# The end of a two-layer transformer kernel: last chunk's stages ahead of the batches, result places computed in the last score steps, dense units turned a step later

## The chip, the cores and the metric

The kernel runs on one core of one Trainium2 chip. The metric is device time in microseconds (us) of one execution. The engines are named as in the profile: PE (TensorE matmul), PEld (its weight loads), DVE (VectorE), ACT (ScalarE), POOL (GpSimd) and SP (SyncE, which here issues most DMAs). Each engine works through its own instructions in the order in which the program lists them, and waits at an instruction until its inputs and its buffer are there.

## The reference

The input x has 32 sequences of 256 tokens with 128 features. Two layers follow. Each has a self-attention with 16 heads of 8, and then a mixture of 16 experts of which every token takes the best two; layer norms are modulated per sequence, and each half is gated per sequence and added to x. Cut to the second layer's expert part, which the change concerns:

```python
h = layernorm(x) * (1 + cb) + sb
probs = softmax(h @ router_w.T)                 # 16 experts
top_w, top_i = top_k(probs, 2); top_w /= sum(top_w)
for e in range(16):                             # 64 wide
    out += dense_w[:, e] * ((silu(h @ Wg[e]) * (h @ Wu[e])) @ Wd[e])
out += sigmoid(h @ shared_gate_w) * ((silu(h @ Sg) * (h @ Su)) @ Sd)   # 256 wide
x = x + gb * out
```

Everything is computed in float32.

## The kernel before

The 32 sequences are cut into 16 chunks of two sequences (512 tokens). Two layers make 32 chunks of work, C = 0 to 31; C from 16 on is layer 1. The program is one long loop over steps `t`, written out by hand. A chunk takes 16 steps, in which its attention scores are formed twice (for the maxima, and 12 steps later for the exponentials) and multiplied by the values. The scores end at step `NU` = 512; the loop runs on to `END`, which is about 70 steps later.

Within each step the program emits instructions in a fixed order: score and value matmuls; early planned work (`early`); the stages of the chunk that fall on this place in its 16 steps, for the engines other than PE (`on_others`, then `on_others_late`); planned work that comes behind (`behind_`); the chunk's stage on PE (`on_pe`); and late planned work (`late`), which is mostly PE's. `plan(at, where, f, ...)` puts a call into one of the three planned lists. So the position of a call within a step is its position in each engine's queue.

The stages of a chunk after its scores are, on the non-PE side: copy of the values' product (`copy_pv`, ACT), division by the softmax sums (`divide`, DVE: rec L981 and cx L983), `keep_ctx` (ACT L998), `add_o` (DVE L1013), statistics and norm (`stats`, `norm`, ACT L551), the modulation (`h_rows`, POOL L614 and L616), `keep_h` (ACT L637), and the routing. On PE they alternate with `turn_ctx` (cT, L989), `proj_o` (y, L1003), `turn_b` (xnT_b, L563) and `logits` (lp, L643).

The experts' work is sparse for most chunks. Tokens are scattered by expert into an array `hs` in HBM, by groups of chunks (8, 8, 8 and 6 chunks; the last group is chunks 24 to 29). Each group is then worked off in batches of four tiles of 128 rows: load the rows (`load`, SP L1315), turn them (t, L1358), multiply by the up weights (gu, L1371), activation (`act_1`, ACT L1394, DVE L1395 and L1396), turn again (aT, L1414), copy (`keep_act`, ACT L1418), multiply by the down weights (y, L1425), weigh (yw, DVE L1436) and store to `ys` (SP L1443). The last group has 16 batches, one in each step from about 511, in the order turn, up, down, turn_act on PE. When all of a group is stored, POOL gathers each token's two rows back with indirect DMAs (L855, eight for a chunk), from places that `find_slots` computes on DVE: L817 twice, L823, L830 and L832, which writes the tile gslot. The sums are gated and added to x (`y_summed` L870, `y_gated` L874, `y_added` L878) and stored (L1642). The gate is loaded by SP into a single buffer (yg, L800).

The two last chunks, 30 (`DENSE`) and 31 (`LAST`), go another way: all experts are computed for all their tokens, as 40 units (2 chunks, 4 token tiles, 5 parts: four of four experts each, and the shared expert). The units begin two steps before the last batch is done. A unit has a product on PE (`dense_up`, du, L1471 or L1474) into one of four banks, a tanh (ACT L1489), three DVE operations (L1490, L1492, L1493, or L1490 and L1495 for the shared part), a turn on PE (`dense_turn`, L1499) back into its bank, a copy (`dense_keep`, ACT L1505) and the down product (`dense_down`, L1514). `dense_add` (L1525, L1526) adds a finished token tile to x and SP stores it (L1528).

Of the kernel before, what the change touches and what calls it, by code (L numbers as in the profile page):

```python
# [9 lines left out]
F32 = mybir.dt.float32  # L10
U32 = mybir.dt.uint32
# [6 lines left out]
B, S, D = 32, 256, 128  # L18
H, HD = 16, 8
E, FI, FS = 16, 64, 256  # L20
EPS = 1e-5
P = 128
# [3 lines left out]
NT = CT // P  # L26
# [4 lines left out]
G, J, R = 2, 8, 16  # L31
# [50 lines left out]
def two_layers(  # L82
# [37 lines left out]
    work = ctx.enter_context(tc.tile_pool(name="work", bufs=2))  # L120
    once = ctx.enter_context(tc.tile_pool(name="once", bufs=1))
    small = ctx.enter_context(tc.tile_pool(name="small", bufs=2))
# [11 lines left out]
    groups = [Group(k) for k in range(len(GROUPS))]  # L134
# [10 lines left out]
    early, behind_, late = {}, {}, {}  # L145

    def plan(at, where_, f, *args):
        where_.setdefault(at, []).append((f, args))
# [238 lines left out]
    def where(C):  # L387

        return divmod(C, NCHUNK)

    def group_of(C):
        return next((g for g in groups if g.first <= C < g.end), None)
# [12 lines left out]
    NU = CHUNKS * CB * G * 4  # L405
# [399 lines left out]
    shifts, gslots = {}, {}  # L805
# [6 lines left out]
    def find_slots(C):  # L812

        l, c = where(C)
        oh = small.tile([P, 2, NT, E], F32, tag="oh2", bufs=1, name=f"oh2_{C}")
        for n in range(2):
            nc.vector.tensor_tensor(  # L817
                oh[:, n],
                iota_e,
                chosen[:, c, :, n : n + 1].to_broadcast([P, NT, E]),  # L820
                ALU.is_equal,
            )
        nc.vector.tensor_tensor(  # L823
            oh,
            oh,
            shifts[group_of(C).k].unsqueeze(1).unsqueeze(1).to_broadcast([P, 2, NT, E]),
            ALU.mult,
        )
        sh = small.tile([P, 2, NT], F32, tag="sh", name=f"sh_{C}")
        nc.vector.tensor_reduce(sh, oh, AX.X, ALU.add)  # L830
        gslots[C] = small.tile([P, 2, NT], U32, tag="gslot", bufs=8, name=f"gslot_{C}")
        nc.vector.tensor_tensor(gslots[C], sh, rowed[:, c], ALU.add)  # L832

    yt2s, gathered_from = {}, {}
# [266 lines left out]
    def do(t, what, dc, *rest):  # L1101
        C = t // 16 + dc
        if 0 <= C < CHUNKS:
            what(C, *rest)
# [346 lines left out]
    UNITS = [(C, t, part) for C in range(DENSE, CHUNKS) for t in range(NT) for part in range(5)]  # L1451
# [24 lines left out]
    def dense_act(n):  # L1476
        C, t, part = UNITS[n]
        p = dn_ps[n]
        s = once.tile([P, G, S], F32, tag="cu", name=f"ds{n}").rearrange("p g s -> p (g s)")[:, :FS]
        a_ = work.tile([P, G, S], F32, tag="q2", name=f"da{n}").rearrange("p g s -> p (g s)")[:, :FS]  # L1480
        dn_as[n] = a_
        if part < 4:
            gu = p.rearrange("p (e n i) -> p e n i", n=2, i=FI)
            gate, upv = gu[:, :, 0, :], gu[:, :, 1, :]
            s, a_ = (v.rearrange("p (e i) -> p e i", i=FI) for v in (s, a_))
            w = everyone[C][:, t, 4 * part : 4 * part + 4].unsqueeze(2).to_broadcast([P, 4, FI])
        else:
            gate, upv = p[:, :FS], p[:, FS:]
        nc.scalar.activation(s, gate, AF.Tanh, scale=0.5)  # L1489
        nc.vector.scalar_tensor_tensor(a_, s, 1.0, gate, ALU.add, ALU.mult)  # L1490
        if part < 4:
            nc.vector.tensor_tensor(a_, upv, a_, ALU.mult)  # L1492
            nc.vector.tensor_tensor(a_, a_, w, ALU.mult)  # L1493
        else:
            nc.vector.scalar_tensor_tensor(a_, a_, zts[C][:, t, :], upv, ALU.mult, ALU.mult)  # L1495
# [153 lines left out]
    END_ROOM = (2, 2, 2, 2, 2, 2, 1, 0, 1, 0, 0, 2, 2, 2, 2, 2)  # L1649
    END = 0  # L1650

    at, left = 16 * (CHUNKS - 3) + 4, 0
    for g in groups:
        if g.l == 0:
            continue
        if at < done[g.k] + 2:
            at, left = done[g.k] + 2, 0
        for C in range(g.first, g.end):
            plan(NU + 2 * (C - g.first) if g is groups[-1] else at, behind_, find_slots, C)
            for n in range(8):  # L1660
                while left == 0:
                    at += 1
                    if at < NU:
                        left = ROOM[at % 16]
                    else:
                        left = END_ROOM[at - NU] if at < NU + len(END_ROOM) else 1 + (at % 5 == 0)
                left -= 1
                if n == 0:
                    gathered_from[C] = at
                plan(at, behind_, gather, C, n)  # L1670
            plan(at, behind_, y_gate, C)
            later = 6 if g is groups[-1] else 3
            plan(at + later - 1, behind_, y_summed, C)
            plan(at + later, behind_, y_gated, C)
            plan(at + later + 1, behind_, y_added, C)
            plan(at + later + 2, early, store, C)
            END = max(END, at + later + 3)

    plan(16 * LAST + 2, early, pairs_weights)
    R0, D0 = 16 * (LAST + 1) + 13, done[groups[-1].k] - 2  # L1680
    plan(16 * (LAST + 1) + 5, behind_, dense_gates, DENSE)
    plan(D0, behind_, dense_gates, LAST)
    for n in range(len(UNITS) + 4):
        for f, where_, after in (
            (dense_turn, late, 2),
            (dense_down, late, 3),
            (dense_up, late, 0),
            (dense_keep, early, 3),
            (dense_act, early, 1),
        ):  # L1690
            if 0 <= n - after < len(UNITS):
                plan(D0 + n, where_, f, n - after)
        if n >= 4 and UNITS[n - 4][2] == 4:
            plan(D0 + n, early, dense_add, *UNITS[n - 4][:2])
    END = max(END, D0 + len(UNITS) + 4)
    for at, where_ in ((0, early), (0, behind_), (1, early), (1, early), (1, behind_), (1, behind_)):
        plan(R0 + at, where_, lambda: next(routes[LAST]))

# [46 lines left out]

    for t in range(-AHEAD, END):
        place = t % 16
        if t == NU:
            scores_pool.__exit__(None, None, None)
            endp.append(ctx.enter_context(end_pool))  # L1750
        m2, after2 = weigh_parts(t) if 0 <= t < NU else ([], None)

        if t < 0:
            if t % 2 == 0:
                (m1, after1), (m2, held_back) = (
                    maxima_parts(
                        t + n + AHEAD, pair(f"s1_{t + n + AHEAD}") if n else None
                    )
                    for n in range(2)
                )  # L1760
            else:
                m1, after1 = [], held_back
        else:
            m1, after1 = maxima_parts(t + AHEAD) if t + AHEAD < NU else ([], None)
        for n in range(NQ):
            for out_, lhs, rhs in m1[2 * n : 2 * n + 2] + m2[2 * n : 2 * n + 2]:
                nc.tensor.matmul(out_, lhs, rhs, start=True, stop=True)  # L1767
        if place in on_pe_mid:
            do(t, *on_pe_mid[place])
        then = [others(p) for others, p in after_job]  # L1770
        after_job.clear()
        for f, args in early.get(t, ()):
            f(*args)
        for stage in on_others.get(place, ()):
            if t < 0 and (stage[0], t // 16 + stage[1]) == (keep_v, 0):
                continue
            do(t, *stage)
        if after1:
            after1()
        if after2:  # L1780
            after2()
        for f in then:
            if f:
                f()
        for stage in on_others_late.get(place, ()):
            if t < 0 and stage[0] in (stats, power, offset) and t // 16 + stage[1] == 1:
                continue
            do(t, *stage)
        for f, args in behind_.get(t, ()):
            f(*args)  # L1790
        if 2 <= t <= NU + 1:
            values(t // 2 * 2 - 1, t % 2)
        if place in on_pe and not (t < 0 and on_pe[place][0] is proj_v):
            do(t, *on_pe[place])
        for g in groups:

            if t == 16 * (g.end + 1) + 1:
                jobs[:0] = table_jobs(g)
        if place == 12 and NCHUNK <= t // 16 - 1 < DENSE:
            jobs.extend(shared_jobs(t // 16 - 1))  # L1800
        for f, args in late.get(t, ()):
            f(*args)
        if t >= NU and jobs or t >= 0 and jobs and t % 3 == 0:
            name, pe, others = jobs.pop(0)
            p = bank("a", name) if t < NU else end_bank(3, name)
            pe(p)
            after_job.append((others, p))
# [102 lines left out]
```

## Time and profile before

| what | time |
|---|---|
| median of 3 runs | 1776.97 us (1776.05 to 1781.66) |
| the profiled execution | 1783.62 us |
| its span, first to last instruction | 1781.9 us |
| mean granted TensorE clock | 0.972 |
| PE busy | 1679.8 us (94%) |
| DVE busy | 1343.5 us (75%) |
| ACT busy | 971.6 us (55%) |
| POOL busy | 717.7 us (40%) |

The rest of the numbers come from one profiled execution, with times counted from its first instruction. A line of the timeline shows the start, the time from the first start to the last end of the merged instructions, the engine, the line of the kernel, the operation, its output and inputs with shapes, and how many were merged. In brackets stands the idle time of the engine just before, and what ended it. A line by stretches shows the stretch, its length, the busy time and the number of instructions of PE, PEld, DVE, ACT and POOL, the granted TensorE clock, the busy share of the DMA engines and what they moved in GB/s. The chain that ended last is followed back from the last instruction, at each step to what released it.

### The profile page before, as it was taken

What the parts mean: (1) busy time and instruction counts of PE and PEld (TensorE: products, weight loads), DVE (VectorE), ACT (ScalarE), POOL (GpSimd) and SP (SyncE); (2) the same over time, 40 slices, a digit from 0 to 9 for tenths busy, and PEclk for the clock granted to TensorE, in tenths of its full rate; (3) what the DMA queues carried; (4) which work ended last, traced back from release to release, by engine and by line L of the source; (5) the groups of instructions that cost most, each with busy time, mean ns of one, the idle gap of its engine ahead of it and who ended that gap; (6) DMA issues with size and microseconds to landing.
All of it is one profiled execution on the core that took longest, in us unless ns stands there. A gap on an engine that the chain in (4) does not pass through costs nothing.

```text
span 1781.9 us, 45990 instructions
## 1 busy us (share of the span) xinstructions
PE 1679.8 (94%) x17025; PEld 1040.6 (58%) x17025; DVE 1343.5 (75%) x3811; ACT 971.6 (55%) x1602; POOL 717.7 (40%) x697
## 2 busy tenths in 40 slices
PE   7999999999999999999999999999999999998897
PEld 3555555555656665555666665555656666546754
DVE  6677777777768877786888887888776767755677
ACT  2566666666546666664546555655665455543333
POOL 2013333332212335664334344555543343553374
PEclk9999999999999999998999999999999999978899
DMA  2132112112445432223444544122332331234532
GB/s 58 41 77 67 47 49 63 49 45 63 105 108 126 106 91 57 56 59 79 111 112 114 95 96 103 45 50 63 99 85 74 81 96 51 69 110 107 139 93 81
DMA packets 211137, 143.38 MB, mean 80 GB/s; under 512 B 33410, under 2 KB 195618, under 8 KB 210914
## 3 DMA queue, kind: packets, MB, share of 16 engines
q1 hardware_dynamic: 187954, 108.65, 24.5%
q0 software_dynamic: 22528, 31.61, 7.1%
q8 instruction: 138, 2.26, 0.5%
q14 instruction: 85, 0.69, 0.1%
q10 hardware_dynamic: 432, 0.16, 0.0%
HBM read 76.91 MB, written 44.62 MB: 68 GB/s over the span
## 4 chain that ended last, share of the span: by engine, by line
PE 42%; DVE 13%; ACT 3%; issue 2%; DMA 2%; POOL 1%; SPq 0%; DVEq 0%; POOLq 0%; ACTq 0%
PE s L1767 14%; PE pv L1186 6%; DVE mpad L1150 3%; PE y L1425 3%; PE gu L1371 3%; PE su L1550 1%; PE aT L1414 1%; PE so L1567 1%; PE t L1358 1%; PE lp L643 1%; PE sg L1539 1%; PE vp L950 1%; PE tp L971 1%; ACT ex L1174 1%; DVE yw L1436 1%
## 5 line engine op out<-in xcount | busy, mean ns | idle before, releaser
L1174 ACT ACTIVATE ex<-s 128x1024 f32<-128x1024 f32 x512 | 523.4, 1022 | 473.9 <-PE s L1767 471.1
L1150 DVE TENSOR_REDUCE mpad<-s 128x2 f32<-128x512 f32 x1018 | 656.9, 688 | 159.1 <-PE s L1767 156.3
L1767 PE MATMUL s<-ka,qa 32*128 32x256 f32 x4096 | 639.4, 414 | 20.5 <-DVE mpad L1150 18.5
L1767 PE MATMUL s<-qa,ka 32*128 32x256 f32 x4096 | 591.2, 406 | 6.6 <-DMA qa<-mc 3.6
L1767 PEld LDWEIGHTS s<-ka,qa 32*128 32x128 f32 x4096 | 376.5, 189 | 198.4 <-DVE mpad L1150 75.1
L1767 PEld LDWEIGHTS s<-qa,ka 32*128 32x128 f32 x4096 | 357.6, 187 | 31.2 <-ACT ex L1174 15.6
L855 POOL DMA_INDIRECT yt<-ys,gslot x220 | 253.5, 1152 | 206.3 <-DVE gslot L832 68.6
L1186 PE MATMUL pv<-ex,vaug 128*32 128x256 f32 x4096 | 332.9, 397 | 3.2 <-ACT cu L964 1.3
L786 POOL DMA_INDIRECT hs<-hrow,slot x240 | 248.0, 1033 | 199.5 <-DVE yt L874 84.1
L1186 PEld LDWEIGHTS pv<-ex,vaug 128*32 128x32 f32 x4096 | 81.2, 109 | 170.1 <-issue 153.4
L769 POOL TENSOR_TENSOR oh<-oh,at 128x128 f32<-128x128 f32 x30 | 14.7, 490 | 257.3 <-DVE at L767 257.3
L534 POOL TENSOR_TENSOR rstd_a<-ve_a,mhalf 128x4 f32<-128x4 f32 x32 | 33.7, 1054 | 174.7 <-DVE ve_a L527 172.1
L1425 PE MATMUL y<-wdd,aT 65*128 (+1 forms) x608 | 89.5, 291 | 0.7 <-ACT aT L1418 0.7
L1425 PEld LDWEIGHTS y<-wdd,aT 65*128 65x128 f32 (+1 forms) x608 | 77.2, 198 | 17.6 <-issue 12.3
L1364 ACT COPY xT<-t 128x512 f32<-128x512 f32 x76 | 44.4, 584 | 78.7 <-PE t L1358 46.4
L1371 PE MATMUL gu<-wgu,xT 128*128 x608 | 86.1, 288 | 0.0
L1371 PEld LDWEIGHTS gu<-wgu,xT 128*128 128x128 f32 x608 | 79.8, 205 | 0.1
L1418 ACT COPY aT<-aT 64x512 f32<-64x512 f32 x76 | 43.9, 577 | 52.2 <-PE aT L1414 51.1
L614 POOL TENSOR_TENSOR xn_b<-xn_b,bc 128x512 f32<-128x512 f32 x32 | 41.0, 1281 | 73.1 <-ACT xn_b L551 73.1
L607 POOL TENSOR_TENSOR wog<-wo,bc 128x256 f32<-128x256 f32 x32 | 31.7, 989 | 82.7 <-DMA bc<-rows 46.2
L551 ACT ACTIVATE xn_a<-x,off_a,rstd_a 128x128 f32<-128x128 f32 x128 | 56.2, 491 | 12.6 <-DVE off_a L540 12.6
L1436 DVE TENSOR_TENSOR yw<-y,hl 128x512 f32<-128x512 f32 x76 | 52.0, 684 | 9.0 <-PE y L1425 8.7
(226 smaller groups left out, 2227.7 us busy)
## 6 DMA issues: line engine op xcount, KB each, us to landing
hl<-hs SPq DMA_DIRECT2D x304, 64.5 KB
ys<-yw SPq DMA_DIRECT2D x76, 256.0 KB
bc<-rows SPq DMA_DIRECT2D x32, 384.0 KB
bg<-bgt SPq DMA_DIRECT2D x160, 64.0 KB
ka<-kc SPq DMA_DIRECT2D x128, 64.0 KB
qa<-qc SPq DMA_DIRECT2D x64, 128.0 KB
hs<-empty SPq DMA_DIRECT2D x68, 64.5 KB
x<-in_x_dram SPq DMA_DIRECT2D x16, 256.0 KB
```

What stands on the lines that cost most here:

```text
L551: nc.scalar.activation(xns[C, ab][:, t, :], xs[c][:, t, :], AF.Identity, bias=off[:, t : t + 1], scale=rstd[:, t : t + 1],)
L786: ins = nc.gpsimd.indirect_dma_start(out=hs[g.k], out_offset=bass.IndirectOffsetOnAxis(ap=slots[C][:, k, t : t + 1], axis=0), in_=hrows[C] ...
L855: ins = nc.gpsimd.indirect_dma_start(out=(yt2s if apart_ else yts)[C][:, t, :], out_offset=None, in_=ys[g.k], in_offset=bass.IndirectOffse ...
L1150: nc.vector.tensor_reduce(to_, sc_, AX.X, ALU.max, negate=True)
L1174: nc.scalar.activation(ex, sc, AF.Exp)
L1186: nc.tensor.matmul(pvs[C, i][j * W : (j + 1) * W, s, :], vaug[C % 2][:, i * NQ + n, s * ST + j, a, :], ex[:, j % 2, n * S : (n + 1) * S], ...
L1364: nc.scalar.copy(xTs[k, b], pst[k, b])
L1371: nc.tensor.matmul(gus[k, b][:, q, :], xTs[k, b][:, q, :], weights[g.l][0][:, bass.ds(es[k, b][q], P)], start=True, stop=True,)
L1418: nc.scalar.copy(aT[:FI], pst["a", g.k, b][:FI])
L1425: nc.tensor.matmul(yps[k, b][:, q, :], aT[:kk, q, :], weights[g.l][1][:kk, bass.ds(es[k, b][q], P)], start=True, stop=True,)
L1436: nc.vector.tensor_tensor(yws[k, b], yps[k, b], hl[k, b][:, :, H_W : H_W + 1].to_broadcast([P, NT, D]), ALU.mult)
L1767: nc.tensor.matmul(out_, lhs, rhs, start=True, stop=True)
```

## The change

Three things change, and two pools.

First, the result places of the last group. `find_slots` for chunks 24 to 29 was planned at steps 512, 514, ... 522. It is now planned at steps 506 to 511, one each. The pool of gslot tiles grows from 8 to 14.

Second, from step 512 on, the early planned work (the batches', the units' and the last routing) is emitted after the stages of `on_others` instead of ahead of them. Before step 512 the order is as it was.

Third, the units. A unit's turn comes three steps after its product instead of two, its copy and down product four instead of three, and `dense_add` five instead of four. The tile da moves to another pool and has three buffers instead of two. The loop's end moves by one step where the units set it.

No instruction is added or taken away.

```diff
@@ find_slots
-        gslots[C] = small.tile([P, 2, NT], U32, tag="gslot", bufs=8, name=f"gslot_{C}")
+        gslots[C] = small.tile([P, 2, NT], U32, tag="gslot", bufs=14, name=f"gslot_{C}")
@@ dense_act
-        a_ = work.tile([P, G, S], F32, tag="q2", name=f"da{n}").rearrange("p g s -> p (g s)")[:, :FS]
+        a_ = once.tile([P, G, S], F32, tag="q2", bufs=3, name=f"da{n}").rearrange("p g s -> p (g s)")[:, :FS]
@@ the plan of the gathers
-            plan(NU + 2 * (C - g.first) if g is groups[-1] else at, behind_, find_slots, C)
+            plan(NU - 6 + C - g.first if g is groups[-1] else at, behind_, find_slots, C)
@@ the plan of the units
-    for n in range(len(UNITS) + 4):
+    for n in range(len(UNITS) + 5):
         for f, where_, after in (
-            (dense_turn, late, 2),
-            (dense_down, late, 3),
+            (dense_turn, late, 3),
+            (dense_down, late, 4),
             (dense_up, late, 0),
-            (dense_keep, early, 3),
+            (dense_keep, early, 4),
             (dense_act, early, 1),
         ):
             if 0 <= n - after < len(UNITS):
                 plan(D0 + n, where_, f, n - after)
-        if n >= 4 and UNITS[n - 4][2] == 4:
-            plan(D0 + n, early, dense_add, *UNITS[n - 4][:2])
-    END = max(END, D0 + len(UNITS) + 4)
+        if n >= 5 and UNITS[n - 5][2] == 4:
+            plan(D0 + n, early, dense_add, *UNITS[n - 5][:2])
+    END = max(END, D0 + len(UNITS) + 5)
@@ the loop over steps
-        for f, args in early.get(t, ()):
-            f(*args)
+
+        planned = early.get(t, ())
+        if t < NU:
+            for f, args in planned:
+                f(*args)
+            planned = ()
         for stage in on_others.get(place, ()):
             if t < 0 and (stage[0], t // 16 + stage[1]) == (keep_v, 0):
                 continue
             do(t, *stage)
+        for f, args in planned:
+            f(*args)
```

## The prediction

> **What bounds the kernel now.** I read the page first (the busy shares, the clock row, the chain that ended last), then busy time by stretch, then TensorE's own timeline of the last 180 us, then the other engines' timelines around each gap in it. The instruction order of the two kernels on every engine is the same up to step 506 (about 1595 us; steps run to 511 with scores). So only the end can move, and I cut it into stretches. The columns are: length; busy PE, PEld, DVE, ACT, POOL; granted clock; DMA share; GB/s.
>
> ```profile
> 1595.00:1613.40 18.40, 17.84 (x116) 8.84 (x112) 5.12 (x21) 8.02 (x13) 10.56 (x11) 0.74 0.60 152
> 1613.40:1692.50 79.10, 67.49 (x441) 59.09 (x438) 50.93 (x166) 26.30 (x57) 30.62 (x32) 0.81 0.44 119
> 1700.00:1772.00 72.00, 64.98 (x329) 39.36 (x328) 57.85 (x138) 27.93 (x77) 47.75 (x48) 1.00 0.31 84
> ```
>
> TensorE is the bound all along, but in the stretch of the 16 batches (1613 to 1692) it has gaps and a clock of 0.81, and in that of the dense units (1700 to 1772) it idles 7 us at full clock. Its timeline names the gaps:
>
> ```profile
> 1624.24 0.63 PE L1414 MATMUL aT<-ident,a 128*64 128x128 f32 x4
> 1629.08 0.66 PE L989 MATMUL cT<-ident,cx 128*128 128x128 f32 x2 [4.21 <-DVE cx L983]
> ...
> 1660.61 0.63 PE L1414 MATMUL aT<-ident,a 128*64 128x128 f32 x4
> 1662.94 1.11 PE L563 MATMUL xnT_b<-ident,hrow 128*128 128x128 f32 x4 [1.70 <-POOL hrow L616]
> ...
> 1669.18 1.79 PE L643 MATMUL lp<-wr1g,hT_b 128*128 128x17 f32 x8 [1.21 <-ACT hT_b L637]
> ...
> 1688.37 0.60 PE L1414 MATMUL aT<-ident,a 128*64 128x128 f32 x4 [2.40 <-DVE a L1396]
> 1689.69 2.00 PE L1425 MATMUL y<-wdd,aT 64*128 x8 [0.72 <-ACT aT L1418]
> ```
>
> The first three wait for a stage of the last chunk that another engine runs behind batch work. The last waits for routing work that stands ahead of a batch. VectorE before the first gap:
>
> ```profile
> 1626.65 0.17 DVE L832 TENSOR_TENSOR gslot<-sh,rowed 128x8 uint32<-128x8 f32 x1
> 1626.73 0.42 DVE L1395 SCALAR_TENSOR_TENSOR a<-s,gu 128x256 f32<-128x256 f32 x1
> 1627.53 0.68 DVE L1436 TENSOR_TENSOR yw<-y,hl 128x512 f32<-128x512 f32 x1
> 1628.51 0.42 DVE L983 TENSOR_TENSOR cx<-tp,rec 128x256 f32<-128x256 f32 x1
> ```
>
> Its input tp had been there since 1621.9. A gap costs more than itself: the clock falls to half afterwards. Cut into stretches of 3.41 us, the clock is constant within each of these:
>
> ```profile
> 1624.95:1628.36 3.41, 0.00 (x0) 0.00 (x0) 3.20 (x12) 0.58 (x1) 1.53 (x2) 1.00 0.30 93
> 1628.36:1631.77 3.41, 2.42 (x11) 2.08 (x12) 0.54 (x2) 0.00 (x0) 2.50 (x4) 0.50 0.66 177
> 1659.08:1662.49 3.41, 2.16 (x17) 1.65 (x15) 3.38 (x6) 2.07 (x5) 2.56 (x2) 1.00 0.69 170
> ```
>
> After each of these full-clock stretches with 1.2 us or more of idle comes one at 0.50. Half clock then held four stretches from 1628.36, one from 1662.49, three from 1669.31 and three from 1689.79. In the dense stretch one unit looks like this:
>
> ```profile
> 1704.57 1.02 PE L1471 MATMUL du<-wgu,hT_b 128*128 128x512 f32 x2
> 1705.43 0.40 PE L1499 MATMUL du<-ident,da 128*128 128x128 f32 x2
> ...
> 1706.12 1.02 PE L1471 MATMUL du<-wgu,hT_b 128*128 128x512 f32 x2
> 1707.52 0.44 PE L1499 MATMUL du<-ident,da 128*128 128x128 f32 x2 [0.38 <-DVE da L1493]
> ```
>
> The product of 1704.57 is turned at 1707.52: 2.95 us through one tanh and three VectorE operations, while PE has work of its own for 2.55 (0.86 product, 0.24 turn, 0.45 down, 0.86 product, with the small issue gaps).
>
> **The change part by part.** I follow PE from mark to mark; PE's own order is the same until the dense units, so a mark moves only by what released it.
>
> *Result places moved.* Six times L817 (two), L823, L830, L832, 1.12 us of VectorE each (1624.49 to 1625.61), go from among the batches into steps 506 to 511. VectorE is busy there 5.12 of 18.40 us, so 6.7 more fit. One lands next to POOL's L614/L616 (1595.86 to 1598.46). Where this meeting occurs now, at 1660.34, the two L817 took 1.42 instead of 0.35 and L823 1.24 instead of 0.29. So up to 2 us of delay there; the transpose that needs POOL's result starts at 1600.90, 2.4 us after it. Cost 0, and more only if POOL lost over 2.4. The larger gslot pool adds buffers and no instruction. At step 512 the moved work frees 1.2 us of VectorE, but the one at step 511 takes it back.
>
> *Last chunk's stages first.* (a) The three small "every" operations (0.65) now precede the first batch's activation, whose result PE takes at 1619.04, 0.3 after it is ready: +0.4. Then rec and cx (0.35 + 0.42) follow the places of chunk 21 directly, ahead of one find_slots (1.12), two a (0.80) and yw (0.60), 2.5 in all: cx ends at 1626.4 + 0.4 = 1626.8 and cT starts at 1626.9 instead of 1629.08: **-2.2**. A gap of 1.6 us stays (PE is done at 1624.87 + 0.4).
> (b) From cT to xnT_b took 33.86 us. At full clock a batch step takes 2.97 (t 0.44, gu 0.89, y 1.08, aT 0.56 in the chain), the cT 0.27, the output projection L1003 half of L1567's 1.80 = 0.9: eight steps are 23.7, with these 24.9. ScalarE copies ctxT at once, so the 1.04 gap before L1003 (1636.83) goes. The gap before xnT_b goes too: the second pair of norms runs at 1656.7 rather than 1658.82, POOL starts 2.1 earlier and is done 0.4 to 0.9 before PE asks at 1661.24. So -8.95 if no half clock follows the 1.6 us gap, and as little as -3.25 if it costs what it does now (14.13 us against 7.11 for the first two steps, less 1.31 of gaps: 5.7). 1.6 us lies above the 1.2 that sufficed; the projection and turns that follow, without the gap in them, should end it earlier, after some 2.3 stretches of 3.41 at half speed, 3.9: **-5.0**.
> (c) xnT_b to lp: 6.24 becomes 0.5 + 2.97 = 3.45, since hT_b is copied ahead of the batches' ACT work: **-2.8**.
> (d) lp (about 1.0 at full clock, as at 1605.73) to the turn at 1680.85: 11.67 becomes 1.0 + 2 x 2.97 = 6.95, because the 1.2 us gap that brought half clock is gone: **-4.7**.
> (e) From there to 1700.25 nothing is reordered. The routing of the last chunk (1682.52 to 1687.36, 4.9 us of VectorE) still stands ahead of a batch: gaps of 2.4 and 0.72 and three half-clock stretches stay: 0. Bounds: 3 us either way.
>
> What is late next in this part: SP. Its six last row loads took 1646.81 to 1667.47, 3.44 a batch against PE's 2.97, with the queue full. Load 10 waits for the third yw, some 9 us earlier than now, so the last lands at about 1660, and PE wants it at 1666: covered by about 6 us. The yw store and yg loads that stand between keep their places.
>
> *Units turned a step on.* PE gets 1.55 us more cover per unit; da has three buffers, enough since a turn three steps on frees the one used four steps on; the four product banks still free in the same PE step. From 1700.25 to the last down product (1772.05) are 71.8 us. PE's own work is 37 products (29 at 0.87, 8 at 0.93), 39 turns at 0.26, 40 downs at 0.445: 60.6. VectorE's in that time, by pitch: 30 x 1.25 + 8 x 0.85 + 7 x 0.53 (dense_add) + 16 x 0.60 (chunk sums) = 57.7. The two are near equal and bunch, and the last unit still runs through ScalarE, VectorE and PE (3.1 us from the end of its product at 1768.94, of which PE can fill 2.4): I take 64.3, **-7.5**. Bounds: 0, if VectorE's bunching sets the pace, and -11, PE's work bare.
>
> *The end.* From the last down product to the end, 9.85 us: the last yg load is issued on SP behind the store of the last dense rows in both kernels (1772.75, then 1773.36), lands 3.0 later, then L874, L878 and a store of 4.0. VectorE's L874 now precedes dense_add; the store does not move: 0. The 48 gathers, started by the last yw's store (1700.59), ran until 1762.65; they start 14.7 earlier and the last sum is reached 22.2 earlier, so their 11 us of slack shrink to about 3.
>
> **The sum**: 2.2 + 5.0 + 2.8 + 4.7 + 7.5 = 22.2 us off a span of 1781.9. The profiled execution took 1783.62 (1.72 around the span), 6.65 above the median, so I take the difference off the median: 1776.97 - 22.2, about **1755 us**.
>
> **The rivals.** *Full clock after the first gap.* The two stretches with the smallest gap that brought half clock hold 1.2 us of idle; one with 0.4 (1682.96 to 1686.38) did not. The 1.6 us may be split between two stretches. Then (b) is -8.95: 1751.
> [...]
>
> *The dense units do not gain.* The chain from 1702 to 1722 runs on VectorE mostly (da and the chunk sums back to back, 1707.39 to 1713.55). If that is the true pace, only (a) to (d) remain: 1776.97 - 14.7 = 1762. Against: VectorE is busy 57.85 of 72.
>
> *The change does not do what it says.* If each gap that closes opens at the next late stage (the SP loads, the last chunk's routing), and VectorE holds the units, under 5.3 us are left: 1772 to 1782. Against it speak PE's full-clock steps at 1643 to 1661 without a gap.
>
> *Slower, by the gathers.* POOL's 48 gathers start at 1685.9 and share the time with a busier VectorE. The last must land (2.4), be summed, gated and added (2.1) and stored (4.0). That ends 5.3 us later than now if the pitch exceeds (1787.2 - 8.5 - 1685.9) / 48 = 1.93 us; at 2.1 it gives 1790. The pitch now is 1.29; only 6 of 48 took over 1.10 instead of 0.94.
> [...]
>
> **How the numbers follow.** Forecast 0.50, full clock 0.18, no gain in the units 0.18, not as said 0.06, slower 0.08. 0.3% (5.3 us) is about what a measurement of this kernel can tell from no change. So faster 0.86, same 0.06, slower 0.08. The range reaches from (b) at -8.95, (e) at -3 and the units at -11 (1744, rounded inwards to 1746) to the units at 0, (b) at -3.25 and (e) at +3 (-10: 1767, rounded outwards to 1768).
>
> **What would show it.** cT waits under 2 us for cx; no wait before L1003, xnT_b and lp; half clock from the last of these to 1680 gone; the aT gap of about 2.4 still there; the waits of du turns for da nearly gone and VectorE above 85% busy between first and last unit; the last yg load again the last wait. Wrong would be: PE waiting for hl rows, POOL gathers ending after the units, or a clock at half through the batches.

## The result, and the profile after

The changed kernel takes 1757.14 us (median of 4 runs, 1751.82 to 1764.46) against 1779.11 us for the kernel before beside it (4 runs, 1776.05 to 1781.66). The ratio is 0.9873, with a 95% interval of 0.984 to 0.9907, that is 16.5 to 28.5 us less. 1755 was predicted.

The profiled execution of the changed kernel is the shortest of its four: 1751.82 us, span 1750.0. That of the kernel before (1783.62) lay above all four of its runs. So the two traces differ by 31.9 us of span and the medians by 22. 4.7 of the 31.9 us come ahead of the first mark of the table, some 4 of them ahead of step 506, where both kernels still have the same instructions in the same order. The rest divides over PE's own marks, each named by what PE starts there:

| stretch on PE | before, us | after, us | difference | predicted |
|---|---|---|---|---|
| last L1567 of the chunk ahead to cT (a) | 9.61 | 7.09 | -2.5 | -2.2 |
| cT to xnT_b (b) | 33.86 | 26.81 | -7.05 | -5.0 |
| xnT_b to lp (c) | 6.24 | 3.42 | -2.8 | -2.8 |
| lp to the last batch's turn (d) | 11.67 | 7.11 | -4.6 | -4.7 |
| that turn to the fifth unit (e) | 22.07 | 19.05 | -3.0 | 0 |
| fifth unit to the last down product (units) | 69.15 | 60.14 | -9.0 | -7.5 |
| last down product to the end (tail) | 9.83 | 11.58 | +1.75 | 0 |
| sum | 162.43 | 135.20 | -27.2 | -22.2 |

Busy time by stretch in the changed kernel, with the columns that the prediction gives. The first line is its batches, the second the first units, the third the other units:

```profile
1608.40:1671.40 63.00, 57.71 (x441) 50.50 (x438) 44.37 (x141) 26.18 (x57) 30.87 (x32) 0.94 0.60 158
1671.40:1676.30 4.90, 4.90 (x16) 2.27 (x16) 2.51 (x6) 1.34 (x3) 2.83 (x3) 0.78 0.58 140
1676.30:1736.00 59.70, 58.51 (x320) 40.17 (x319) 56.41 (x138) 24.72 (x77) 43.13 (x45) 1.00 0.37 98
```

The batches took 79.1 us at a clock of 0.81; now they take 63 at 0.94. PE does the units almost without a pause (58.5 of 59.7 us), and VectorE is busy for 56.41 of 59.70, 94%. PE's timeline in the batches shows which waits are left:

```profile
1621.89 0.41 PE L989 MATMUL cT<-ident,cx 128*128 128x128 f32 x2 [1.73 <-DVE cx L983]
...
1627.00 1.06 PE L1003 MATMUL y<-wog,ctxT 128*128 128x128 f32 x8
...
1648.70 0.60 PE L563 MATMUL xnT_b<-ident,hrow 128*128 128x128 f32 x4
...
1652.12 0.96 PE L643 MATMUL lp<-wr1g,hT_b 128*128 128x17 f32 x8
...
1666.74 1.03 PE L1414 MATMUL aT<-ident,a 128*64 128x128 f32 x4 [2.34 <-DVE a L1396]
...
1668.50 2.07 PE L1425 MATMUL y<-wdd,aT 64*128 x8 [0.72 <-ACT aT L1418]
```

The projection, xnT_b and lp, which waited before, have no bracket now. The cT waits 1.73 instead of 4.21 us, and the wait behind the last chunk's routing is still 2.34. The two longest waits of PE and PEld for the units' da in the list of waits (in total, times, longest, us) were these before:

```profile
PEld du L1499 <- DVE da L1493: 28.9, 31, 1.3
PE du L1499 <- DVE da L1493: 6.0, 15, 0.6
```

and these after. Of PE's 6.0 us one wait of 0.74 is left; two others, of 0.23 and 0.49, are for the da of a shared part. All but the 0.23 come behind the last product. The last line is new:

```profile
PEld du L1499 <- DVE da L1493: 7.7, 15, 0.9
PE du L1499 <- DVE da L1493: 0.7, 1, 0.7
PE du L1499 <- DVE da L1495: 0.7, 2, 0.5
DVE yt L870 <- DMA yt<-ys,gslot: 4.2, 1, 4.2
```

It stands at the end of the timeline:

```profile
1739.54 0.39 SPq L800 DMA_DIRECT2D yg<-rows  x1
1739.68 0.94 POOL L855 DMA_INDIRECT yt<-ys,gslot  x1 [0.30 <-issue]
1743.91 0.69 DVE L870 TENSOR_TENSOR yt<-yt 128x512 f32<-128x512 f32 x1 [4.24 <-DMA yt<-ys,gslot]
1744.63 0.69 DVE L874 TENSOR_TENSOR yt<-yt,yg 128x512 f32<-128x512 f32 x1
1745.36 0.69 DVE L878 TENSOR_TENSOR x<-yt,x 128x512 f32<-128x512 f32 x1
```

The last gather is issued 1.26 us after the end of the last down product (1738.42), and VectorE waits 4.24 us for it. The yg load, issued at the same time, is waited for by nobody.

### The profile page after: what moved, and what is told of

The parts are those of the page before. It is cut to its first block, busy times and chain, and to the rows that moved or that the text cites. A ratio compares the mean times of both kernels' runs of the same rounds, so it can differ in the third digit from the quotient of the medians.

```text
span 1750.0 us, 45956 instructions
## 1 busy us (share of the span) xinstructions
PE 1657.0 (95%) x17025; PEld 1028.1 (59%) x17025; DVE 1339.9 (77%) x3811; ACT 968.3 (55%) x1602; POOL 716.6 (41%) x697
## 4 chain that ended last, share of the span: by engine, by line
PE 40%; DVE 12%; POOL 3%; ACT 3%; issue 3%; DMA 2%; SPq 0%; POOLq 0%; DVEq 0%; ACTq 0%
PE s L1768 14%; PE pv L1186 6%; DVE mpad L1150 4%; PE y L1425 3%; PE gu L1371 3%; POOL yt L855 2%; PE so L1567 1%; PE aT L1414 1%; PE su L1550 1%; PE sg L1539 1%; PE t L1358 1%; PE lp L643 1%; DMA yt<-ys,gslot 1%; PE vp L950 1%; PE tp L971 1%
## 5 line engine op out<-in xcount | busy, mean ns | idle before, releaser
L1768 PEld LDWEIGHTS s<-qa,ka 32*128 32x128 f32 x4096 | 355.6, 186 | 31.9 <-ACT ex L1174 16.0
L769 POOL TENSOR_TENSOR oh<-oh,at 128x128 f32<-128x128 f32 x30 | 14.7, 490 | 256.8 <-DVE at L767 256.8
L1371 PE MATMUL gu<-wgu,xT 128*128 x608 | 82.2, 279 | 0.0
L1371 PEld LDWEIGHTS gu<-wgu,xT 128*128 128x128 f32 x608 | 75.6, 195 | 0.0
L551 ACT ACTIVATE xn_a<-x,off_a,rstd_a 128x128 f32<-128x128 f32 x128 | 56.2, 491 | 12.5 <-DVE off_a L540 12.3
```

Source lines behind the costliest of these rows:

```text
L551: nc.scalar.activation(xns[C, ab][:, t, :], xs[c][:, t, :], AF.Identity, bias=off[:, t : t + 1], scale=rstd[:, t : t + 1],)
L1371: nc.tensor.matmul(gus[k, b][:, q, :], xTs[k, b][:, q, :], weights[g.l][0][:, bass.ds(es[k, b][q], P)], start=True, stop=True,)
```

## The experiments

The kernels below ran on four other chips. On these the kernel before took 1972 to 1996 us instead of 1777, and in every kernel's trace ScalarE waits there, for up to 18 us at a time, behind work of PE that is recorded as done. These waits are called stops here; the last section says what the trace shows of them. So these runs are read in two ways: their ratios, and inside their traces by waits and marks that lie away from those waits. "Theory A" is the prediction's account. The expectations' numbers come from the first comparison; the waits that they name were met, while the gains in total mostly came out smaller, and stretches that hold such a stop longer.

**The places alone, the order alone.** `places_only` moves `find_slots` and enlarges gslot, and leaves the rest as before:

```
-plan(NU + 2 * (C - g.first) if g is groups[-1] else at, behind_, find_slots, C)
+plan(NU - 6 + C - g.first if g is groups[-1] else at, behind_, find_slots, C)
-tag="gslot", bufs=8
+tag="gslot", bufs=14
```

> The kernel before with only the result places of the last group computed in steps 506 to 511 (and 14 gslot buffers). Theory A: the gap before cT falls from 4.2 to about 3.1 us, still with half clock behind it; the gaps before the projection, xnT_b and lp stay; 1 to 3 us less, ratio 0.999. Rival D (the places held VectorE): the gap before cT under 1.5 us and 10 us less in all.

`stages_only` changes the order from step 512 alone:

```
-        for f, args in early.get(t, ()):
-            f(*args)
+        planned = early.get(t, ())
+        if t < NU:
+            for f, args in planned:
+                f(*args)
+            planned = ()
         for stage in on_others.get(place, ()):
             ...
             do(t, *stage)
+        for f, args in planned:
+            f(*args)
```

> The kernel before with only the order changed: from step 512 on the last chunk's stages ahead of planned work. Theory A (gaps of PE come from the order, and half clock from the gaps): the gap before cT is about 2.7 us (one find_slots of 1.1 more than in the changed kernel), no gap before the projection, xnT_b and lp, half clock only after cT and after the routing; first batch turn to first du product 64 to 68 us instead of 79, ratio about 0.993. Rival D (the result places were what held VectorE): more than 73 us.

`all_but_places` is the changed kernel with the two lines of `places_only` as they were before.

> The changed kernel with the result places left where they were before (steps 512 to 522, 8 gslot buffers). Theory A: the gap before cT about 2.7 us instead of 1.7, else as the changed kernel: 1 to 3 us more than it, ratio to before 0.988 to 0.990. Rival D: most of the gain gone, ratio above 0.994.

Measured: places_only 0.9996 (0.996 to 1.0032), stages_only 0.995 (0.9922 to 0.9977), all_but_places 0.9953 (0.9926 to 0.998). PE's timeline of places_only:

```profile
1779.48 0.66 PE L989 MATMUL cT<-ident,cx 128*128 128x128 f32 x2 [3.12 <-DVE cx L983]
...
1813.22 0.66 PE L563 MATMUL xnT_b<-ident,hrow 128*128 128x128 f32 x4 [1.73 <-POOL hrow L616]
```

and of stages_only:

```profile
1780.72 0.66 PE L989 MATMUL cT<-ident,cx 128*128 128x128 f32 x2 [2.85 <-DVE cx L983]
...
1785.55 1.06 PE L1003 MATMUL y<-wog,ctxT 128*128 128x128 f32 x8
...
1811.40 0.60 PE L563 MATMUL xnT_b<-ident,hrow 128*128 128x128 f32 x4
```

The wait ahead of cT is 4.2 us with neither part (4.20 and 4.24 in the two runs of the units alone, below), 3.12 with the places, 2.85 with the order, and 1.73 with both (in both traces of the changed kernel, and in two others). The places take away 1.1 us in either case, which is the 1.12 us of VectorE that the prediction counted for one `find_slots`. They take no more than that, and no ratio shows it alone. The waits ahead of the projection, xnT_b and lp go with the order: xnT_b to lp takes 3.41 us wherever the order is changed and ScalarE does not stop in that stretch, and 5.6 to 12.0 in the four kernels that keep the old one (9.8 and more with a stop in it).

The stretch from the first batch's turn to the first unit, which several expectations name, held stops in every run. The eight runs with the new order, those below included, took 72 to 83 us for it, and the four with the old one 83 to 90 (62.9 and 79.1 in the first comparison). In stages_only it took 80.4, where 64 to 68 were expected and more than 73 was the mark of rival D; so this stretch decides nothing, and the waits inside it speak for theory A. By its ratio all_but_places, too, met rival D (above 0.994), but the changed kernel itself gives 0.9954 on such a chip (`changed_again`, below), so that run shows no loss without the places.

**The units.** `units_only` turns the units a step on in the kernel before, with the third da buffer:

```
-    for n in range(len(UNITS) + 4):
+    for n in range(len(UNITS) + 5):
-            (dense_turn, late, 2),
-            (dense_down, late, 3),
+            (dense_turn, late, 3),
+            (dense_down, late, 4),
-            (dense_keep, early, 3),
+            (dense_keep, early, 4),
-        if n >= 4 and UNITS[n - 4][2] == 4:
+        if n >= 5 and UNITS[n - 5][2] == 4:
 ...
-a_ = work.tile([P, G, S], F32, tag="q2", name=...)
+a_ = once.tile([P, G, S], F32, tag="q2", bufs=3, name=...)
```

> The kernel before with the units alone a step on (turn, copy, down product and adding one step later, da with three buffers). Theory A (a unit's turn came too early for its chain through ACT and DVE): first batch turn to first du product unchanged at about 79 us; first du product to last down product 67 to 69 instead of 79.6; the end then set by the 48 gathers, which start as before, so about 10 us less in all (ratio 0.994). Rival B (DVE sets the pace of the units): less than 2 us.

`da_buffers_only` has only the last two lines of it.

> The kernel before with only the tile da in three buffers of another pool; the units' steps as before. Theory A: no change (ratio 1.000), PE still waits for da at its turns, 1.85 us a unit. Rival C (the second buffer was what held the units): first du to last down product under 72 us, ratio 0.995.

`units_again` is units_only once more, beside `all_but_units`, which has the order and the places and neither the later turn nor the third buffer.

> The kernel before with the units turned a step on, a second time, beside the rest of the change alone. In five consecutive units without a stall of ScalarE, theory A (the wait of the du turns for da was the pace) expects 7.6 us a group of five against 9.1 in the kernel before; theory B (VectorE was the pace) 9.1 in both. On a chip where ScalarE does not stall: the last down product some 12 us earlier than before, but the gathers start where they did, so they, not the last yg load, end last, and the whole gains only 9 to 11 us, ratio about 0.994 to 0.995; if the gathers have slack, 12 us or more, 0.993. On a chip with ScalarE stalls among the units: 0.9976 as the first time, and 9.7 us from the last down product to the end.

> The changed kernel without the units turned a step on: the order of the stages and the result places alone. Theory A: cT waits 1.7 us for cx, no gap before the projection, xnT_b and lp, the aT gap of 2.4 stays, du turns wait 0.6 for da as in the kernel before, five unstalled units take 9.1 us, and the end (last down product to end) takes 9.7 to 10 us, the yg load last. On a chip where ScalarE does not stall: 14 to 16 us less, ratio about 0.991 to 0.992, so that this and the units alone add up to the whole change or to a little less. With stalls: 0.994 to 0.996. Rival: the two parts need each other, and this alone gains under 5 us, ratio above 0.997.

Measured: units_only 0.9976 (0.9945 to 1.0008), units_again 0.9979 (0.995 to 1.0007), da_buffers_only 1.0023 (0.9988 to 1.0058), all_but_units 0.9975 (0.9952 to 0.9999). Five consecutive units (four products of four experts, one of the shared) that fall between ScalarE's stops, in units_again:

```profile
1930.58 0.60 PE L1474 MATMUL du<-sg,hT_b 128*128 128x256 f32 x2
...
1932.97 0.38 PE L1499 MATMUL du<-ident,da 128*128 128x128 f32 x2
1933.64 1.02 PE L1471 MATMUL du<-wgu,hT_b 128*128 128x512 f32 x2
1934.50 0.38 PE L1499 MATMUL du<-ident,da 128*128 128x128 f32 x2
...
1938.22 0.60 PE L1474 MATMUL du<-sg,hT_b 128*128 128x256 f32 x2
```

and in all_but_units:

```profile
1924.90 0.60 PE L1474 MATMUL du<-sg,hT_b 128*128 128x256 f32 x2
...
1926.55 0.44 PE L1499 MATMUL du<-ident,da 128*128 128x128 f32 x2 [0.62 <-DVE da L1493]
...
1930.15 0.44 PE L1499 MATMUL du<-ident,da 128*128 128x128 f32 x2 [0.32 <-DVE da L1493]
...
1934.44 0.44 PE L1499 MATMUL du<-ident,da 128*128 128x128 f32 x2 [1.02 <-DVE da L1493]
1935.16 0.60 PE L1474 MATMUL du<-sg,hT_b 128*128 128x256 f32 x2
```

From one shared product to the next it is 7.64 us with the later turn and no wait, and 10.26 here without it. The shortest such group is 7.63 us in each of the nine traces with the later turn and 8.96 to 9.12 in the five without it, those of the first comparison included (there 9.0 to 9.6 before and 7.6 to 8.2 after, in all seven groups). So the wait for da was the pace, the later turn with the third buffer takes it away, and the third buffer alone takes away nothing; the later turn without that buffer was not run. That is 1.5 us for five units, some 12 for forty.

The whole kernel shows some 4 to 5 us of this on these chips, with intervals that reach 1, and the traces say where the units' time goes: the 35 units from the fifth to the last take 98.3 and 100.3 us in units_only and units_again, and 96 to 102 in all eight runs with the later turn, against 100 to 103 in the four with the old one (before and after in the first comparison: 65.0 and 54.7). From the ninth to the fifteenth unit alone go 40 to 45 us in every kernel there, against 11.4 and 9.2, and there lie ScalarE's longest stops. So the ratios of these four runs do not measure what the units are worth where ScalarE does not stop. The expectation for all_but_units of 0.994 to 0.996 was missed: 0.9975 lies on the rival's side of 0.997, and the interval covers both, so on these chips that run decides nothing by its ratio. With units_again it multiplies to 0.9954, the changed kernel's own ratio on such a chip (`changed_again`, below), as parts that add up would. Its waits do: 1.73 ahead of cT, none ahead of xnT_b and lp, 2.39 ahead of aT, which is what theory A expected.

**Two further steps**, on the waits that the change leaves. `routing_spread` spreads the last chunk's routing over later steps:

```
-    for at, where_ in ((0, early), (0, behind_), (1, early), (1, early), (1, behind_), (1, behind_)):
+    for at, where_ in ((0, early), (0, behind_), (2, behind_), (3, behind_), (4, behind_), (5, behind_)):
```

> The changed kernel with the last chunk's routing spread over steps 525 to 530, behind the batches' work, instead of over 525 and 526. Theory A: the gap of 2.3 us before the turn of batch 14 and that of 0.7 behind it go, and so does half clock after them; first batch turn to first du product 59 to 60 us instead of 63; the gathers, now the last bound, start as much earlier: 3 to 5 us less than the changed kernel, ratio to before about 0.985. Rival E (the gap comes from the batch's own chain): no change against the changed kernel.

`pe_stage_later` puts the chunk's stage on PE behind the batch's work in the last steps:

```
-        if place in on_pe and ...:
+        if t < NU + 2 and place in on_pe and ...:
             do(t, *on_pe[place])
         ...
         for f, args in late.get(t, ()):
             f(*args)
+        if t >= NU + 2 and place in on_pe:
+            do(t, *on_pe[place])
```

> The changed kernel with the last chunk's own PE stage put behind the batch's products in each step from 514 on, so that cT has a step of cover. Theory A: no gap before cT, no half clock behind it at full-clock steps of 2.97 us; first batch turn to first du product 59 to 60 us instead of 63; 2 to 4 us less than the changed kernel. Rival F (half clock after cT comes with what PE runs there, not with the gap): the gap gone and still a half-clock stretch before the projection.

`both_further` has both.

> Routing spread and the last chunk's PE stage behind the batch's products together, on the changed kernel. Theory A: no gap over 0.5 us and no half clock from the first batch to the last unit; first batch turn to first du product about 56 us instead of 63; the end set by the gathers from start to finish (first gather to end about 71 us): 5 to 8 us less than the changed kernel, ratio to before about 0.983.

Measured, beside all_but_places (0.9953) on the same chip: 0.9956 (0.9928 to 0.9984), 0.9929 (0.9895 to 0.9963) and 0.996 (0.9932 to 0.9989). In routing_spread PE's timeline at the place of the 2.34 us wait reads:

```profile
1852.08 0.63 PE L1414 MATMUL aT<-ident,a 128*64 128x128 f32 x4
1853.43 1.16 PE L1425 MATMUL y<-wdd,aT 64*128 x8 [0.72 <-issue]
1854.51 0.63 PE L1414 MATMUL aT<-ident,a 128*64 128x128 f32 x4
1854.98 1.02 PE L1471 MATMUL du<-wgu,hT_b 128*128 128x512 f32 x2
```

and in pe_stage_later, around cT:

```profile
1796.62 0.60 PE L1414 MATMUL aT<-ident,a 128*64 128x128 f32 x4
1797.05 0.38 PE L989 MATMUL cT<-ident,cx 128*128 128x128 f32 x2
1798.38 0.66 PE L1358 MATMUL t<-ident,hl 128*128 128x128 f32 x4 [0.95 <-ACT ctxT L998]
```

Each takes away the wait that it was made for: the last turn to the first unit falls from 11.7 to 7.95 us, and cT no longer waits. So rivals E and F are out: the gap goes with the routing, and in pe_stage_later the clock stays full from 1788.7 to 1829.7, across cT and the projection at 1801.41. No ratio of these three can be told from the changed kernel's own; the intervals reach 5 to 7 us to either side, as much as most of the gains that were expected. both_further took 72.1 us from the first batch's turn to the first unit instead of 56, with two stops of 6.8 and 7.3 us in it and half clock behind them.

`changed_again` is the changed kernel, and `both_again` is both_further, on another chip, to see whether these differ there.

> The changed kernel once more. The four single-part kernels and the four on top of the change ran on chips where every kernel, the one before too, takes some 11% longer, and ScalarE waits up to 18 us in the dense units for nothing that the trace shows. Theory G (these waits lie at the same units whatever the order, and swallow what the units gain): on such a chip 8 to 12 us less than before, ratio 0.994 to 0.996, no such waits in the batches beyond one; on a chip without them about 22 us less, ratio 0.987. Rival H (the gain is as large on every chip): 20 us or more less, ratio under 0.990, with the waits there.

> Routing spread and the last chunk's PE stage behind the batch's products, on the changed kernel, once more. On a chip without the long ScalarE waits: no gap over 0.5 us between the first batch and the last unit, first gather to end about 71 us, 5 to 8 us less than the changed kernel. On a chip with them: within 4 us of the changed kernel either way.

Measured: 0.9954 (0.9924 to 0.9984) and 0.9949 (0.9918 to 0.9981). The first is what theory G expected; rival H's ratio, under 0.990, lies outside its interval. The two cannot be told apart, so no kernel here is shown to beat the changed one. On a chip without the stops the further steps were not measured.

## Why the prediction was right, and where it was not

The direction and the size (22.2 predicted, 22.0 measured between medians) hold, and the parts (a), (c) and (d) came out to 0.3 us. Their cause is shown by the runs: the order takes the waits ahead of the projection, xnT_b and lp, and the 4.2 us ahead of cT fall by 1.1 through the places and 1.35 to 1.4 through the order. The agreement to 0.2 us is luck, though: the measurement's interval is 12 us wide, and in the profiled execution the same terms sum to 27.2, with (b), (e) and the units too small by 2.05, 3.0 and 1.5 and the end too small by 1.75 the other way. No trace of a slower execution of the changed kernel on that chip exists, so what they lack against the fastest is not divided here.

- **(b), -5.0, measured -7.05.** The step "some 2.3 stretches of 3.41 at half speed" was the mis-sized term. One such stretch followed. 24.9 us of full-clock work and half of 3.41 make 26.6, and 26.81 were measured. The rival *full clock after the first gap* did not occur here; one trace of another kernel shows it (last section).
- **(e), 0 with bounds of 3, measured -3.0.** The gaps of 2.34 and 0.72 stayed, as said. "Three half-clock stretches stay" failed: two followed (1666.74 to 1673.57), and half clock ended 2.2 us behind the start of the first unit instead of 7.6 (1671.36, before 1692.48). About 0.7 of the 3.0 is no gain: with the later turn one turn and one down product fewer (0.26 and 0.445) stand ahead of the fifth unit, and the units' row holds them.
- **Units, -7.5, measured -9.0.** The mechanism is shown, by units_again against all_but_units. The size was off since PE got closer to its bare pace than the allowance for VectorE's bunching: 54.68 us for 35 units are 1.562 a unit, where its own work was counted at 0.87 + 0.26 + 0.445 = 1.575 for a product of four experts. (The 7.5 counts from 1700.25, some two units ahead of the mark of the table.) At 94% VectorE hardly held PE up (0.23 us of waits for da ahead of the last product). The rival *the dense units do not gain* is out.
- **The end, 0, measured +1.75.** "The store does not move: 0" failed at the gathers. Their slack of 11 us was said to shrink to 3; it shrank to nothing. The gathers start at 1679.46 instead of 1700.59, 21.1 us earlier, and the last is issued 22.0 earlier (1739.68, before 1761.71), but the last down product is done 33.6 earlier (1738.42, before 1772.05). The prediction had set an end that comes 22.2 earlier against gathers that start 14.7 earlier. Of both it had too little, and the difference between them was 12.5 instead of 7.5: the very time that PE gained from the first unit on. POOL's pitch stayed at 1.28 (60.22 us for 47 steps), far from the 1.93 of the *slower* rival, so the mechanism was there and the price small. That the gathers end after the units is one of the signs which the prediction itself named for being wrong, and the yg load was not the last wait, as it had said. In the runs on the other chips the units take 96 us or more, the gathers are done long before, and the yg load is waited for last again (2.70 us ahead of the last L874 in units_again, 1.84 in all_but_units) with 9.9 to 10.0 from the last down product to the end.
- **The places, 0**: the ratio of places_only agrees, 0.9996.

## What to carry to other kernels

A gap of PE is worth here what it costs itself and half of each stretch of half clock behind it (26.81 us from cT to xnT_b, where full-clock work of 24.9 and half of one stretch of 3.41 make 26.6). Count the first exactly, and give the second a range, since the same gap of 1.73 us gave none or one here. When a stage becomes faster, time from its start what runs beside it at a pace of its own (here 48 gathers at 1.28 us), because it becomes the end as soon as the stage needs less than it does. And where the engine that a unit waits for is busy in bunches, a step more between product and use can be worth more than its mean load suggests: here VectorE was busy for 57.85 of 72.00 us, a further buffer alone gave nothing (da_buffers_only, 1.0023), and the later turn brought PE to its bare pace (1.562 us a unit).

## What the runs showed of the hardware

**The same gap can bring half clock or not.** The wait of 1.73 us ahead of cT occurs in four traces of this study. The clock changes on a grid of 3.41 us (in the two traces of the first comparison all 27 and 21 changes lie whole multiples of 3.41 us apart); these are the stretches around that wait, first in the changed kernel of the first comparison:

```profile
1618.96:1622.37 3.41, 1.60 (x12) 1.01 (x10) 3.24 (x11) 1.13 (x4) 0.52 (x1) 1.00 0.31 91
1622.37:1625.78 3.41, 3.34 (x15) 3.14 (x16) 0.75 (x2) 0.79 (x2) 2.50 (x4) 0.50 0.46 125
```

then routing_spread:

```profile
1791.35:1794.76 3.41, 1.78 (x14) 1.32 (x12) 3.27 (x11) 1.45 (x3) 0.00 (x0) 1.00 0.25 75
1794.76:1798.17 3.41, 3.31 (x15) 2.85 (x15) 1.30 (x3) 0.37 (x1) 2.74 (x3) 0.50 0.33 98
```

and all_but_units:

```profile
1787.35:1790.76 3.41, 2.24 (x18) 1.73 (x16) 3.24 (x11) 1.45 (x3) 0.00 (x0) 1.00 0.13 38
1790.76:1794.18 3.42, 2.71 (x21) 2.41 (x22) 1.76 (x4) 1.06 (x3) 2.29 (x3) 1.00 0.39 114
1794.18:1797.59 3.41, 3.08 (x27) 2.77 (x25) 0.00 (x0) 0.18 (x1) 2.50 (x4) 1.00 0.53 138
```

In the first two the gap lies in one stretch (in routing_spread but for its last 0.10), which holds 1.81 and 1.63 us of idle PE, and the next runs at half clock. In the third the same gap falls on both sides of a boundary, 1.17 and 0.71 us of idle, and the clock stays full. In the fourth, changed_again, it lies in one stretch (1783.20 to 1786.61, 1.73 us of idle), and half clock follows. This was the prediction's rival ("the 1.6 us may be split between two stretches"); in these four traces the clock goes with when the gap falls. But no bound on the idle time of one stretch holds throughout: in the kernel before, 1.30 us (993.46 to 996.87) left the clock full and 1.20 (1665.91 to 1669.32) did not; in pe_stage_later 1.76 (1802.36 to 1805.78) left it full; and in the changed kernel half clock follows a stretch with 0.21 (1584.82 to 1588.23). So these traces give no rule for it. How long half clock lasts is not explained either: one stretch after 1.73 and 2.85 us of gap (stages_only), three after 2.85 in all_but_places, two after 4.20 and 4.24 (units_only and units_again), four after 3.12 (places_only), 4.21 (before) and 4.25 (da_buffers_only).

**PE's late signals.** On the four chips of the experiments ScalarE stops before operations whose inputs are recorded as done. From both_further's timeline:

```profile
1885.96 1.91 PE L1471 MATMUL du<-wgu,hT_b 128*128 128x512 f32 x2
1887.66 0.64 PE L1499 MATMUL du<-ident,da 128*128 128x128 f32 x2
...
1894.38 0.38 ACT L1489 ACTIVATE ds<-du 128x256 f32<-128x256 f32 x1 [9.49 <-remote]
...
1900.00 0.37 ACT L1505 COPY dT<-du 128x256 f32<-128x256 f32 x1 [5.23 <-remote]
```

"Remote" means that the view names nothing that released it. The trace holds more than the views print: the times at which each semaphore (a counter that one engine's instructions raise in the trace and other engines' wait for) went up. Both operations start 0.02 us after PE's semaphore went up (1894.36 and 1899.98), though PE's product is recorded to end at 1887.87 and its turn at 1888.30. So it is in all twelve traces of these chips: every wait put down to "remote" there (29 to 48 in each, of VectorE and here and there of PE too) ends with the one semaphore that PE alone raises, 1.5 to 20 us after the last recorded end of a PE instruction that raises it. In the two traces of the first comparison this lag is 0.015 us in the median, and under 0.1 in 99 of 100 cases. So it is PE's signal that comes late, and ScalarE waits for it. Whether PE's work itself took longer than its records show, or only the signal was late, these traces do not tell.

In the list of waits of units_again the longest stop stands last in the line:

```profile
ACT ds L1489 <- remote: 26.6, 3, 17.9
```

The stops fall on about the same units in all twelve runs, around the 9th to 14th and in ten of them again around the 25th to 31st; others lie in the batches and all through the kernel (74 to 145 us of ScalarE's idle time in a trace). None of them is in the two traces of the first comparison, and the changed kernel is in both sets. Why PE's signal is late is open: in both_further no transfer of instructions starts between 1868.1 and 1925.4, where the stops from 1871.7 to 1907.0 lie, and no run here could take them away. The change is worth 1.3% in the first comparison and 0.5% on these chips (changed_again); that the stops make the difference is argued from their place among the units, and not shown.
